# Moving one quarter of the inputs of the eighth step from VectorE to GpSimd in a selective-scan layer

## The chip, the cores and the metric

The kernel runs on one NeuronCore of a Trainium2 chip. Times are device microseconds of one execution of the whole program; "time before" is the median of three runs. The core has TensorE (PE, matrix products into PSUM), VectorE (DVE), ScalarE (ACT), GpSimd (POOL) and SyncE (SP, which here only issues DMA transfers). Each engine works through its own instructions in order and waits on semaphores for the others. SBUF is the working memory of 128 partitions, PSUM the memory that TensorE writes to.

## The reference

The input x has 3 images of 256 channels and 48 x 48 points. Four layers are added to it in turn, each on a group norm of what came before: a block with attention, a convolution with weights mixed from eight experts, a plain convolution, and a selective scan over the 2304 points of each image. Only the last is touched by the change. Cut to what matters:

```python
xz = einsum('blc,dc->bld', layernorm(x), in_proj_w)      # 512 channels d, twice
x_in, z = split(xz, 2)
u = silu(causal_conv4(x_in))
dt_raw, B_ssm, C_ssm = split(einsum('bld,ed->ble', u, x_proj_w))   # 16 + 16 + 16
dt = softplus(einsum('blr,dr->bld', dt_raw, dt_proj_w) + dt_proj_b)
A = -exp(A_log)                                          # 512 x 16
def step(hst, inp):                                      # hst: 512 channels x 16 states
    dA = exp(dt_t[:, :, None] * A)
    hst = hst * dA + dt_t[:, :, None] * B_t[:, None, :] * u_t[:, :, None]
    y_t = einsum('bdn,bn->bd', hst, C_t)
y = (ys + u * D_param) * silu(z)
out = x + einsum('bld,cd->blc', y, out_proj_w)
```

## The kernel before

The program computes the four layers one after the other. The scan layer takes the last two fifths of the time, from about 2008 us on. All numbers are fp32.

**Chunks and steps.** The points of the three images are cut into 18 chunks of 384 (`CH`). A chunk goes through eight steps: four blocks `m` of 128 channels, times two halves `h` of the states. A step holds 128 channels and 8 states, laid out as 128 partitions = 32 channels x 4 states, and along the free dimension a tile `hs` of 2 groups of states `g` x 4 quarters of channels `q` x 384 points. The first step of a chunk is m = 0, h = 0; the eighth is m = 3, h = 1. So the seventh step is m = 3, h = 0.

**A step on each engine.**

- Fills: every (g, q) of `hs` first gets the input of the recurrence, the product dt·u (a quarter of the channels, spread over the partitions) times B. Quarters 0 and 1 are written by VectorE in `fill_upper` (L1765), which reads dt·u from a PSUM tile `ps_r` into which TensorE spread it (`spread_pe`, L1730). One piece, (g, q) = (1, 1) of each second step (h = 1), is written by GpSimd instead (L1779), which reads dt·u from an SBUF tile `dtuq` that DMAs fill (`spread_second`, L1722, a single buffer). Quarters 2 and 3 are written by GpSimd for both groups at once (L1783), from `dtur`, which DMAs fill too (`spread`, L1714, together with `dtr`, the spread dt).
- Decays: ScalarE computes exp(dt·A) for one (g, q) at a time into one of three PSUM slots `ps_da` (L1809).
- Scans: VectorE runs the recurrence over 384 points in place, one (g, q) at a time (L1817), eight scans a step in the order (0,0), (0,1), (1,0), (1,1), (0,2), (0,3), (1,2), (1,3). These are the parts 0 to 7. The decay of part n + 3 is issued behind the scan of part n and needs its slot free.
- GpSimd multiplies the whole `hs` by C into `hc` (`times_c`, L1834; in the very last step VectorE does this, L1828), TensorE sums over the states (`add_states`, L1846 and L1851), and VectorE multiplies by silu(z) (`gate`, L1858).

**Order around the change.** Between two steps the loop issues `fill(s + 1)`, then `times_c(s)`. At a step with h = 0, `fill` has two instructions for VectorE: both groups of that step (128x1536) and already group 0 of the following step (128x768). At a step with h = 1 there is one left for VectorE, (1, 0) (128x384), and L1779 for GpSimd. Then comes L1783 in either case. So VectorE fills for the eighth step in two places: group 0 ahead of the seventh step, (1, 0) ahead of the eighth. `hs` has three buffers, so that GpSimd can fill ahead while VectorE still scans the step before.

A list written out by hand (`plan`, `after`, `gating`) places the preparation of the next two chunks and the output of the one before into half-steps and places within them. Among it are dt·u of the next chunk (`softplus` on ScalarE, L1327 to L1329, and `take_dt` on VectorE, L1343 and L1344, in the sixth and the seventh step), the normalising of the chunk after it (L1246, in the eighth) and the store of the last chunk's output (L1384). `keep_busy` (L1336) issues products on TensorE whose result nobody reads. `first_states` and `last_states` (L1792, L1799) carry states between chunks. At the end of the layer `keep_order` pins the instructions of TensorE, VectorE, ScalarE and GpSimd to the order in which they are written; SyncE is not among them.

The call `fill_upper(s, lo, hi, nq)` covers the groups lo to hi - 1 and the quarters 0 to nq - 1; `b_rows` gives the rows of B for them, each repeated for the quarters. In the code, `chunks[at].second[m]` is `dtuq` and `chunks[at].bc[0]` holds B for the four groups of a channel block, two for each half.

Of the kernel before, what the change touches and what calls it, by code (L numbers as in the profile page):

```python
# [12 lines left out]
ALU = mybir.AluOpType  # L13
# [3 lines left out]
P = 128  # L17
# [8 lines left out]
CH = 384  # L26
# [9 lines left out]
DI = 4  # L36
# [48 lines left out]
def net(  # L85
# [295 lines left out]
    with ExitStack() as l0:  # L381
# [36 lines left out]
        with ExitStack() as p1:  # L418
# [15 lines left out]
            for b in ORDER:  # L434
# [3 lines left out]
                for ct in range(CT):  # L438
                    for j in range(parts):
                        at = slice(j * N // parts, (j + 1) * N // parts)  # L440
# [608 lines left out]
        chunks = [(b, c) for b in ORDER for c in range(NCH)]  # L1049
# [58 lines left out]
    rooms, w3v, chunks, stored = {}, {}, {}, set()  # L1108
# [580 lines left out]
    with ExitStack() as l3:  # L1689
# [60 lines left out]
        def states(s):  # L1750

            if s not in tiles:
                t = scn.tile([P, 2, 4, CH + 4], F32, name="hs", bufs=3)
                tiles[s] = t[:, :, :, 1 : CH + 2]
            return tiles[s]

        def b_rows(s, lo, hi, nq=2):
            at, m, h = steps[s]
            rows = chunks[at].bc[0][:, 2 * h + lo : 2 * h + hi, :]
            return rows.unsqueeze(2).broadcast_to([P, hi - lo, nq, CH])  # L1760

        def fill_upper(s, lo, hi, nq=2):

            k = chunks[steps[s][0]]
            nc.vector.tensor_tensor(  # L1765
                states(s)[:, lo:hi, 0:nq, 1:],
                k.ps[:, 0:nq, :CH].unsqueeze(1).broadcast_to([P, hi - lo, nq, CH]),
                b_rows(s, lo, hi, nq), ALU.mult,
            )

        def fill(s):

            at, m, h = steps[s]
            if h == 0:
                fill_upper(s, 0, 2)
                fill_upper(s + 1, 0, 1)
            else:
                fill_upper(s, 1, 2, 1)
                nc.gpsimd.tensor_tensor(  # L1779
                    states(s)[:, 1, 1, 1:], chunks[at].second[m],  # L1780
                    chunks[at].bc[0][:, 3, :], ALU.mult,
                )
            nc.gpsimd.tensor_tensor(  # L1783
                states(s)[:, :, 2:4, 1:],
                chunks[at].rows[m][1].unsqueeze(1).broadcast_to([P, 2, 2, CH]),
                b_rows(s, 0, 2), ALU.mult,
            )
# [77 lines left out]
        spread_pe(k, 0)  # L1865
        first_states(0)
        fill(0)
        for n in range(3):
            decay(n)
        for s, (at, m, h) in enumerate(steps):  # L1870
# [30 lines left out]
            if s + 1 < len(steps):  # L1901
                fill(s + 1)
# [133 lines left out]
```

## Time and profile before

| What | us |
|---|---|
| median of three runs | 3374.56 (3373.8 to 3378.72) |
| the profiled execution | 3369.03 |
| its span, first to last instruction | 3367.3 |
| busy in the span: TensorE, VectorE | 3151.7 (94%), 2899.6 (86%) |
| busy in the span: ScalarE, GpSimd | 2375.1 (71%), 1335.3 (40%) |
| scans (L1817), 1152 of 936 ns | 1002.6 busy |
| fills by GpSimd of quarters 2 and 3 (L1783), 144 | 418.3 |
| products with C on GpSimd (L1834), 143 | 805.3 |
| fills by GpSimd of (1, 1) (L1779), 72 | about 62 |

Lines of groups give the line of the kernel, the engine, the operation, the tile written and the tiles read, the form and the count, then busy time, the mean of one in ns, and the idle time of that engine just before. Lines of the order in time give start, length, engine, line and operation; a bracket at the end is idle time before it and whose result ended it. Instructions of one kind that follow each other are merged (x2, x6). Lines of waits give who waited for whom, the total in us, how often, and the longest. Consecutive instructions of VectorE overlap by nearly a tenth of a microsecond, so that a scan listed with 936 ns comes every 0.87 us. Tiles that share a room of a former tile appear under two names (`x` or `bc`, `wconv`, `u`).

### The profile page before, as it was taken

The page shows a single profiled execution, that of the slowest core. Times are in us where ns is not written, and L with a number is a line of the kernel's source. Part 1 is how long each engine was busy: PE and PEld are TensorE (multiplying, and loading weights), DVE is VectorE, ACT ScalarE, POOL GpSimd, SP SyncE. Part 2 cuts the span into 40 slices and gives each one's busy share as a digit, 9 for nine tenths or more (in the row PEclk, how much of TensorE's full clock was granted, in tenths as well). Part 3 has the DMA queues.
Part 4 walks back from the last instruction along what each step waited for, and adds up shares of the span by engine and source line. Part 5 has one row for each costly group of instructions (what it writes and reads, how often), then busy time and mean ns, then how long its engine had stood idle before and what let it go on. Part 6 is the DMA issues. An engine that isn't in the chain of part 4 may idle for free.

```text
span 3367.3 us, 54979 instructions
## 1 busy us (share of the span) xinstructions
PE 3151.7 (94%) x21314; PEld 1586.5 (47%) x21314; DVE 2899.6 (86%) x3302; ACT 2375.1 (71%) x3596; POOL 1335.3 (40%) x457
## 2 busy tenths in 40 slices
PE   7999999999999999979999988999999999999985
PEld 4334343452333434547777764444444444444442
DVE  4799989959988997379976459999999999999997
ACT  3688888838888886332233548888888888888874
POOL 0000000000000000220000009999999999999997
PEclk9999999999999999989999999999999999999998
DMA  4000000010000002566611044555545555555552
GB/s 174 23 8 10 8 8 6 8 46 4 8 7 8 10 8 71 193 210 214 218 38 38 19 120 107 125 127 129 143 123 141 133 129 123 130 130 134 135 131 56
DMA packets 182165, 290.84 MB, mean 86 GB/s; under 512 B 34738, under 2 KB 148466, under 8 KB 179971
## 3 DMA queue, kind: packets, MB, share of 16 engines
q1 hardware_dynamic: 168658, 267.15, 29.6%
q10 hardware_dynamic: 13232, 20.06, 1.8%
q8 instruction: 169, 2.77, 0.4%
q14 instruction: 106, 0.86, 0.1%
HBM read 236.24 MB, written 50.64 MB: 85 GB/s over the span
## 4 chain that ended last, share of the span: by engine, by line
PE 52%; DVE 32%; ACT 7%; DMA 4%; issue 4%; SPq 1%; POOL 0%; ACTq 0%; DVEq 0%; POOLq 0%
DVE hs L1817 21%; PE ps_s L638 16%; PE acc L651 14%; PE ps_c L1546 8%; DVE hs L1765 3%; DVE u L296 2%; PE ps_y L462 2%; PE ps_m L665 2%; ACT ps_da L1809 2%; PE ps_s L1031 2%; PE ps_m L711 1%; PE acc L529 1%; PE ps_s L518 1%; DVE ps_g L1343 1%; DMA dtr<-dtd 1%
## 5 line engine op out<-in xcount | busy, mean ns | idle before, releaser
L642 ACT ACTIVATE pt<-ps_s 128x1024 f32<-128x1024 f32 x972 | 942.4, 1022 | 154.8 <-PE ps_s L638 142.1
L1817 DVE TENSOR_TENSOR_SCAN hs<-ps_da,hs 128x385 f32<-128x385 f32 x1152 | 1002.6, 936 | 5.1 <-ACT ps_da L1809 2.4
L857 DVE TENSOR_TENSOR part<-part,pt 128x2048 f32<-128x2048 f32 x396 | 906.6, 2289 | 41.2 <-ACT pt L642 18.5
L1809 ACT ACTIVATE ps_da<-dtr,u 128x384 f32<-128x384 f32 x1152 | 656.3, 582 | 191.3 <-DVE hs L1817 182.7
L164 POOL TENSOR_TENSOR rstd<-ve,mhalf 128x2 f32<-128x2 f32 (+1 forms) x26 | 16.3, 629 | 1473.4 <-DVE ve L162 1473.4
L638 PE MATMUL ps_s<-q,kt 32*128 32x512 f32 (+1 forms) x4320 | 576.4, 592 | 0.1
L651 PE MATMUL acc<-pt,vt 128*32 128x512 f32 (+1 forms) x4320 | 520.9, 561 | 0.2
L1546 PE MATMUL ps_c<-vt,u 128*128 128x288 f32 x1728 | 429.4, 409 | 21.0 <-DVE u L263 21.0
L1834 POOL TENSOR_TENSOR hc<-hs,x 128x3072 f32<-128x3072 f32 x72 | 405.2, 5628 | 30.8 <-DVE hs L1817 26.0
L1834 POOL TENSOR_TENSOR hc<-hs,bc 128x3072 f32<-128x3072 f32 x71 | 400.1, 5635 | 24.7 <-DVE hs L1817 23.0
L1546 PEld LDWEIGHTS ps_c<-vt,u 128*128 128x128 f32 x1728 | 328.9, 191 | 116.6 <-issue 19.8
L638 PEld LDWEIGHTS ps_s<-q,kt 32*128 32x128 f32 x4320 | 195.3, 183 | 199.1 <-issue 120.2
L651 PEld LDWEIGHTS acc<-pt,vt 128*32 128x32 f32 x4320 | 94.4, 108 | 353.4 <-issue 326.7
L1851 PE MATMUL ps_y<-hc,u 128*32 128x384 f32 x2304 | 228.1, 516 | 2.8 <-POOL hc L1834 2.8
L1273 PE MATMUL ps_g<-u 128*128 128x384 f32 x576 | 196.2, 494 | 23.4 <-ACT u L1269 23.4
L1783 POOL TENSOR_TENSOR hs<-dtur,x 128x1536 f32<-128x1536 f32 x72 | 209.0, 2903 | 8.3 <-DMA dtur<-dtud 8.3
L1783 POOL TENSOR_TENSOR hs<-dtur,bc 128x1536 f32<-128x1536 f32 x72 | 209.3, 2907 | 1.3 <-DMA dtuq<-dtud 0.9
L1273 PEld LDWEIGHTS ps_g<-u 128*128 128x128 f32 x576 | 108.8, 191 | 107.7 <-ACT u L1269 34.6
L1336 PE MATMUL ps_r<-hs,ident 128*128 128x128 f32 x864 | 130.9, 292 | 27.3 <-DVE hs L1817 27.2
L1336 PEld LDWEIGHTS ps_r<-hs,ident 128*128 128x128 f32 x864 | 107.6, 192 | 80.8 <-DVE hs L1817 63.0
L1851 PEld LDWEIGHTS ps_y<-hc,u 128*32 128x32 f32 x2304 | 62.0, 112 | 144.5 <-issue 130.4
L1562 ACT COPY cb<-ps_c 128x288 f32<-128x288 f32 x48 | 19.1, 398 | 154.5 <-PE ps_c L1546 140.4
(266 smaller groups left out, 4051.0 us busy)
## 6 DMA issues: line engine op xcount, KB each, us to landing
wconv<-in_we SPq DMA_DIRECT2D x144, 384.0 KB, 4.2
dtr<-dtd SPq DMA_DIRECT2D x288, 192.0 KB, 3.9
dtur<-dtud SPq DMA_DIRECT2D x288, 96.0 KB, 4.3
wconv<-xd SPq DMA_DIRECT2D x36, 384.0 KB, 3.7
x<-bcd SPq DMA_DIRECT2D x72, 192.0 KB, 5.1
dtd<-x SPq DMA_DIRECT2D x36, 384.0 KB, 2.9
dtuq<-dtud SPq DMA_DIRECT2D x288, 48.0 KB, 2.0
bc<-bcd SPq DMA_DIRECT2D x72, 192.0 KB, 4.8
```

Source lines behind the costliest of these rows:

```text
L638: nc.tensor.matmul(s[:, j, cols], kt[r, mt * P : (mt + 1) * P], q[r, :n], start=True, stop=True,)
L642: nc.scalar.activation(p[:, h0 : h0 + 2, :], s, AF.Exp)
L651: nc.tensor.matmul(acc[h * HD : (h + 1) * HD, :n], vt[:, mt, g * P + h * HD : g * P + (h + 1) * HD], p[:, h, cols], start=mt == 0, stop=mt ...
L857: ): nc.vector.tensor_tensor(part, first, p, ALU.add)
L1273: nc.tensor.matmul(bank[m % 2], w3v["taps"][:, m, tap, :], w3v["xi"][:, m % 3, tap : tap + CH], start=tap == 0, stop=tap == DCONV - 1,)
L1336: nc.tensor.matmul(spread_tiles[-1][:, i % 2, CH:], ident, src, start=True, stop=True)
L1546: nc.tensor.matmul(pc[:, :HN], u[:, i, dy, ct, m * P : (m + 1) * P], vt[:, i, ct, dy * TW : dy * TW + HN], start=ct == 0 and dy == 0, stop ...
L1783: nc.gpsimd.tensor_tensor(states(s)[:, :, 2:4, 1:], chunks[at].rows[m][1].unsqueeze(1).broadcast_to([P, 2, 2, CH]), b_rows(s, 0, 2), ALU.mult,
L1809: nc.scalar.activation(slots[n % 3][:, 1 : CH + 1], chunks[at].rows[m][0][:, q, :], AF.Exp, scale=amat[:, col : col + 1],)
L1817: nc.vector.tensor_tensor_scan(b, slots[(8 * s + part) % 3][:, : CH + 1], b, 0.0, ALU.mult, ALU.add)
L1834: nc.gpsimd.tensor_tensor(hc, tiles[s][:, :, :, 1:], cb.broadcast_to([P, 2, 4, CH]), ALU.mult)
L1851: nc.tensor.matmul(k.y_ps[32 * q : 32 * q + 32, :CH], fold, hc[:, g, q, :], start=False, stop=h == 1 and g == 1,)
```

## The change

At the eighth step of each chunk GpSimd fills the second quarter of channels (q = 1) for both groups of states, and VectorE fills only the first. The piece that changes hands is (g, q) = (0, 1), 384 elements in each partition. The call for VectorE ahead of the seventh step covers one quarter instead of two when m is the last block; the instruction for GpSimd ahead of the eighth step covers both groups. At the other steps with h = 1 it covers one group as before, written with a group dimension of one.

```diff
             if h == 0:
                 fill_upper(s, 0, 2)
-                fill_upper(s + 1, 0, 1)
+                fill_upper(s + 1, 0, 1, 1 if m == DI - 1 else 2)
             else:
                 fill_upper(s, 1, 2, 1)
+                lo = 0 if m == DI - 1 else 1
                 nc.gpsimd.tensor_tensor(
-                    states(s)[:, 1, 1, 1:], chunks[at].second[m],
-                    chunks[at].bc[0][:, 3, :], ALU.mult,
+                    states(s)[:, lo:2, 1, 1:],
+                    chunks[at].second[m].unsqueeze(1).broadcast_to([P, 2 - lo, CH]),
+                    chunks[at].bc[0][:, 2 + lo : 4, :], ALU.mult,
                 )
```

## The prediction

> **What bounds the kernel now.** I read the busy shares over the span first, then the totals of one chunk of the scan layer, VectorE's waits there, and the order of time around the edit on VectorE, GpSimd and ScalarE. The edit lies in the scan layer, from about 2008 us to the end. In 40 slices of 84.2 us:
>
> ```profile
> DVE  4799989959988997379976459999999999999997
> ACT  3688888838888886332233548888888888888874
> POOL 0000000000000000220000009999999999999997
> ```
>
> In slices 25 to 39 VectorE and GpSimd both show 9 tenths, so the average of GpSimd over the span (40%) says nothing about its room there. One chunk (eight steps) by itself, from one step's first scan to the same scan a chunk later:
>
> ```profile
> core 0: us, PE busy (x) PEld busy (x) DVE busy (x) ACT busy (x) POOL busy (x), PEclk, DMA share, GB/s
> 2536.79:2611.08 74.29, 68.59 (x348) 36.01 (x347) 73.67 (x90) 62.43 (x123) 71.06 (x21) 1.00 0.55 132
> ```
>
> VectorE is busy 73.67 of 74.29 us, GpSimd 71.06: 0.6 us of room against 3.2. The chunk repeats at 74.3 us (2091.11, 2165.42, 2239.71 and so on). Over sixteen such chunks (2091 to 3278 us) the list of waits has only these for VectorE:
>
> ```profile
> DVE hs L1765 <- ACT wconv L1384: 3.4, 16, 0.2
> DVE ps_g L1343 <- ACT x L1329: 2.8, 16, 0.2
> DVE hs L1817 <- issue: 0.4, 1, 0.4
> ```
>
> That is 0.2 us twice a chunk, none of it for GpSimd. VectorE sets the pace; what it drops counts in full unless something lies within that distance behind it. The place of the edit, in one chunk, on VectorE:
>
> ```profile
> 2514.01 2.62 DVE L1765 TENSOR_TENSOR hs<-ps_r,x 128x1536 f32<-128x1536 f32 x2
> 2516.54 1.80 DVE L1817 TENSOR_TENSOR_SCAN hs<-ps_da,hs 128x385 f32<-128x385 f32 x2
> 2518.25 0.54 DVE L1343 SCALAR_TENSOR_TENSOR ps_g<-ps_g,x 128x384 f32<-128x384 f32 x1
> ...
> 2525.48 0.53 DVE L1765 TENSOR_TENSOR hs<-ps_r,x 128x384 f32<-128x384 f32 x1
> 2525.93 5.40 DVE L1817 TENSOR_TENSOR_SCAN hs<-ps_da,hs 128x385 f32<-128x385 f32 x6
> ```
>
> The first line is the two fills ahead of the seventh step: 1536 elements for that step, 768 for the eighth. The same stretch on GpSimd:
>
> ```profile
> 2513.81 5.63 POOL L1834 TENSOR_TENSOR hc<-hs,x 128x3072 f32<-128x3072 f32 x1 [0.28 <-PE ps_r L1336]
> 2519.40 0.86 POOL L1779 TENSOR_TENSOR hs<-dtuq,x 128x384 f32<-128x384 f32 x1
> 2520.22 2.90 POOL L1783 TENSOR_TENSOR hs<-dtur,x 128x1536 f32<-128x1536 f32 x1
> 2525.74 5.63 POOL L1834 TENSOR_TENSOR hc<-hs,x 128x3072 f32<-128x3072 f32 x1 [2.62 <-DVE hs L1817]
> ```
>
> To be seen: L1779 is the operation that grows, and 2.62 us of GpSimd's 3.2 us of idle time come right behind it, waiting for the seventh step's last scan.
>
> **What the Trainium skill says.** "GPSIMD Engine Reference", 3.1 (Elementwise), gives about 1 cycle an element on VectorE and about 2.6 on GpSimd for an operation with two inputs. At the clocks of the two pages' Specifications (0.96 and 1.2 GHz) that is an estimate of 0.40 us for 384 elements on VectorE and 0.83 on GpSimd. The trace gives 0.418 and 0.68 (below), and these are used. "VectorE: DVE Perf Modes", "Why PSUM operands drop a tier", says that an fp32 operation with a PSUM operand stays at one element a cycle; the fill reads ps_r from PSUM, and 1.05 to 1.09 ns an element agrees. "GPSIMD Engine Reference", 8 (Key points), says that GpSimd contends with VectorE's two-port modes or two SBUF inputs. Scans and fills have one input in PSUM, so more GpSimd time beside them should cost nothing. The trace agrees: the six scans from 2520.37 take 5.20 us, 0.867 each, although GpSimd is busy until 2523.1 and idle after it, and scans fully under GpSimd work keep that pitch.
>
> **The change, part by part.** All of it happens once a chunk, and there are 18 chunks.
>
> *Removed from VectorE.* The second of the two fills (L1765, for the eighth step) goes from 128x768 to 128x384. The view of that line gives 948 ns as its median, which is the 768 form, and 530 as its minimum, the 384 form, so 0.418 us go; from start to start, about 0.86 (2515.7 to 2516.54) less 0.45 (2525.48 to 2525.93) gives 0.41. I take 0.418. The fill ahead of the eighth step (0.53) stays.
>
> *Added to GpSimd.* L1779 goes from 384 to 768 elements. Its own kind of operation costs 865 ns for 384, 2903 for 1536 and 5628 for 3072: (2903 - 865)/1152 = 1.77 ns an element in both steps. So 865 + 384 x 1.77 = 1.54 us, 0.68 more. At the second, fourth and sixth step of a chunk the operation keeps its size and only gets a dimension of one, costed at nothing (at worst some tens of ns, under the same idle time).
>
> *What hides the 0.68.* L1779 starts at 2519.40, ends at 2520.94 instead of 2520.26; L1783 ends at 2523.8 instead of 2523.12. The next operation, L1834, waits for the scan that ends at 2525.5, now 2525.1. So 2.62 - 0.68 - 0.42 = 1.5 us of cover remain; without them, the 0.68 would delay all GpSimd work up to the next chunk.
>
> *Who waits for L1779.* The new part, group 0 second quarter, is scanned as part 1 of the eighth step, at 2525.93 - 0.42 + 0.87 = 2526.4, 5.4 us after 2520.94. L1783's quarters are first due at part 4, at about 2529.0, 5.2 us after 2523.8. No new wait ends there.
>
> *Does the 0.42 get through?* Behind the fill, ScalarE is the nearest:
>
> ```profile
> 2515.96 0.84 ACT L1329 ACTIVATE x<-x 128x768 f32<-128x768 f32 x1
> 2516.71 0.19 ACT L1799 COPY gmat<-hs 128x8 f32<-128x8 f32 x1
> 2517.52 0.58 ACT L1809 ACTIVATE ps_da<-dtr,u 128x384 f32<-128x384 f32 x1 [0.62 <-DVE hs L1817]
> ```
>
> ScalarE waits 0.62 us for the first scan, so it can follow by 0.42 with 0.2 to spare; this wait is 0.62 to 0.72 in all of the first 17 chunks. VectorE's L1343, due at 2517.83 instead of 2518.25, needs L1329, done at 2516.80: 1.0 left. From there ScalarE's decays, TensorE's products and the transfers start from VectorE's results and shift with it, also the two 0.2 us waits, whose ScalarE strings start from waits of 0.26 for a scan. SyncE's queue has the same issues; its L1722 for the next chunk comes at 2527.5, long after L1779 has let go of its only buffer.
>
> *The last chunk* has no preparation of a following one, VectorE is quicker there, and GpSimd works without a gap: L1779 from 3336.54, L1783 from 3337.36, L1834 from 3340.23. With the change L1783 ends at 3336.54 + 1.50 + 2.91 = 3340.95. Part 4 would be due at 3337.67 - 0.42 + 3.46 = 3340.7, now waits for about 3341.0; before it was 3341.1. So 0.1 of the 0.42 remains. L1834 then ends at 3346.5, just ahead of the products at 3346.64 that read it.
>
> *Sum.* 17 x 0.418 + 0.1 = 7.2 us. The profiled execution took 3369.03 us (span 3367.3 and 1.7 around it) and would take 3361.8. The median of the three runs, 3374.56, lies 5.5 above it; I carry the same 7.2 over: 3367.4 us, 0.21% faster.
>
> **The rivals.** *Taken up on the way*: ScalarE has only 0.2 us left behind the fill, and waits of 0.2 on it already stand twice a chunk. If one of its strings were fixed by something else than a scan, a transfer say, VectorE would merely wait longer there. For it: those waits. Against: each string starts from a wait for VectorE. All lost gives 3374.6, half lost 3371.
>
> *Slower, by a wait for VectorE's own fill*: the new L1779 writes one quarter of each of two groups, and between them in memory lies group 1's first quarter, which VectorE fills at 2525.48, ordered ahead of it. If the write counted as one block, L1779 would wait until 2525.6. Then part 1, due at 2526.4, waits for 2527.2, and part 4, due at 2529.8 after that, for L1783 at 2530.05: 0.8 + 0.25 = 1.05 us lost against 0.42 won. That makes +0.63 x 17 = 11 us: 3385. GpSimd would be 4.7 us late too, which its margins of 4 to 5 us just take. It decides from the first overlap counted. Against it: L1783's write spans that very quarter as well and starts at 2520.22 without waiting.
>
> *A longer GpSimd operation* hurts only from 0.68 + 1.5 = 2.2 us of growth, three times the estimate. *Another order of transfers*: SyncE's order isn't among the four that the kernel pins. The tightest transfer, dtr, lands at 2529.3 and ScalarE needs it at 2531.7; beyond 2.4 us a swap would cost, at 1 us a chunk 17 - 7 = 10 us, 3385 again. *That the edit does nothing* is out: it cuts a row with a measured length.
>
> **How the numbers follow.** The forecast has 0.72. Its size lies between 17 x 0.40 = 6.8 and 18 x 0.45 = 8.1 with run noise of about 1 us around it. Taken up wholly or half has 0.15, the wait for the fill 0.08, the other slower ways 0.05. A measurement of this kernel tells about 0.2% (6.75 us) from no change. Four fifths of the forecast's 0.72 lie beyond: faster 0.58; the rest and the absorbed case: same 0.29; slower 0.13. The range goes from 3365 (8.1 and noise) to 3375 (all absorbed).
>
> **What would show it.** Right: the chunk at 73.9 us; L1765 with 54 operations of 128x768 and 90 of 128x384; L1779 at about 1.54 us once a chunk, and the wait of 2.62 us shrunk to 1.5. Wrong: L1779 starting after VectorE's fill, an idle VectorE before part 1 or 4 of the eighth step, or the 0.2 us waits grown to 0.6.

## The result and the profile after

The changed kernel took 3363.81 us (median of 8 executions, 3361.71 to 3369.11) against 3373.61 us of the kernel before beside it (8 executions, 3368.78 to 3378.72). The ratio is 0.9973, with a 95% interval from 0.9964 to 0.9983: 9.1 us faster, between 5.7 and 12.1 (the two medians by themselves are 9.8 apart). That is faster, as forecast, by a little more than the 7.2 us forecast. The median was forecast at 3367.4 us, in a range from 3365 to 3375, and lies 1.2 us below that range.

The profiled execution shows none of it: 3369.11 us, span 3367.4, where the kernel before had 3369.03 and 3367.3. So the time has to be read by stage. The scan layer's first fill (L1765) starts at 2016.82 us in the profile after and at 2008.33 in the one before, although nothing ahead of it was edited; from there to the end it takes 1350.6 against 1359.0 us.

A chunk first. The view of busy times by stretch for the changed kernel, from part 3 of the sixth step (behind `take_dt`) to the same scan a chunk later (columns: stretch, length, busy time of TensorE, its weight loads, VectorE, ScalarE and GpSimd, granted clock, DMA share, GB/s):

```profile
core 0: us, PE busy (x) PEld busy (x) DVE busy (x) ACT busy (x) POOL busy (x), PEclk, DMA share, GB/s
2514.21:2588.11 73.90, 69.35 (x346) 36.09 (x346) 73.28 (x90) 62.45 (x123) 71.70 (x21) 0.98 0.57 135
```

73.90 us where it was 74.29. VectorE has 0.4 us less of work and the same 0.6 us idle, GpSimd 0.6 more. The waits of VectorE over 2091 to 3278 us, same kernel:

```profile
DVE hs L1765 <- ACT wconv L1384: 3.4, 16, 0.2
DVE ps_g L1343 <- ACT x L1329: 2.9, 16, 0.2
DVE hs L1819 <- issue: 0.4, 1, 0.4
```

They are what they were. No new wait has come, and the two of 0.2 us haven't grown. The order in time around the edit, on VectorE, then GpSimd, then ScalarE (lines of the code have moved on by one or two: L1780 is the former L1779, L1785 was L1783, L1819 was L1817, L1811 was L1809, L1836 was L1834):

```profile
2518.93 2.21 DVE L1765 TENSOR_TENSOR hs<-ps_r,x 128x1536 f32<-128x1536 f32 x2
2521.05 1.80 DVE L1819 TENSOR_TENSOR_SCAN hs<-ps_da,hs 128x385 f32<-128x385 f32 x2
2522.77 0.54 DVE L1343 SCALAR_TENSOR_TENSOR ps_g<-ps_g,x 128x384 f32<-128x384 f32 x1
...
2530.45 5.39 DVE L1819 TENSOR_TENSOR_SCAN hs<-ps_da,hs 128x385 f32<-128x385 f32 x6
```

```profile
2518.73 5.63 POOL L1836 TENSOR_TENSOR hc<-hs,x 128x3072 f32<-128x3072 f32 x1 [0.27 <-PE ps_r L1336]
2524.31 1.54 POOL L1780 TENSOR_TENSOR hs<-dtuq,x 128x768 f32<-128x768 f32 x1
2525.81 2.90 POOL L1785 TENSOR_TENSOR hs<-dtur,x 128x1536 f32<-128x1536 f32 x1
2530.25 5.63 POOL L1836 TENSOR_TENSOR hc<-hs,x 128x3072 f32<-128x3072 f32 x1 [1.53 <-DVE hs L1819]
```

```profile
2520.88 0.84 ACT L1329 ACTIVATE x<-x 128x768 f32<-128x768 f32 x1
2521.63 0.19 ACT L1801 COPY gmat<-hs 128x8 f32<-128x8 f32 x1
2522.04 0.58 ACT L1811 ACTIVATE ps_da<-dtr,u 128x384 f32<-128x384 f32 x1 [0.22 <-DVE hs L1819]
```

The two fills take 2.21 instead of 2.62 us. L1780 takes 1.54 us and starts right behind the operation ahead of it, so it doesn't wait for VectorE's fill of the quarter in between, which comes at 2530.00. GpSimd's wait has gone from 2.62 to 1.53, ScalarE's from 0.62 to 0.22.

### The profile page after: what moved, and what is told of

It reads as the page before. It is cut to its first block, busy times and chain, and to the rows that moved or that the text cites. A ratio compares the mean times of both kernels' runs of the same rounds, so it can differ in the third digit from the quotient of the medians.

```text
span 3367.4 us, 54979 instructions
## 1 busy us (share of the span) xinstructions
PE 3159.9 (94%) x21314; PEld 1591.0 (47%) x21314; DVE 2892.8 (86%) x3302; ACT 2376.1 (71%) x3596; POOL 1346.1 (40%) x457
## 4 chain that ended last, share of the span: by engine, by line
PE 52%; DVE 32%; ACT 7%; DMA 5%; issue 4%; SPq 1%; POOL 0%; ACTq 0%; DVEq 0%; POOLq 0%
DVE hs L1819 21%; PE ps_s L638 16%; PE acc L651 14%; PE ps_c L1546 8%; DVE hs L1765 3%; PE ps_s L1031 2%; DVE u L296 2%; PE ps_y L462 2%; ACT ps_da L1811 2%; PE ps_m L665 1%; PE ps_m L711 1%; PE acc L529 1%; PE ps_s L518 1%; DVE ps_g L1343 1%; PE ps_s L578 1%
## 5 line engine op out<-in xcount | busy, mean ns | idle before, releaser
L1819 DVE TENSOR_TENSOR_SCAN hs<-ps_da,hs 128x385 f32<-128x385 f32 x1152 | 1002.1, 935 | 4.2 <-ACT ps_da L1811 1.5
L1811 ACT ACTIVATE ps_da<-dtr,u 128x384 f32<-128x384 f32 x1152 | 656.6, 582 | 184.3 <-DVE hs L1819 175.7
L1836 POOL TENSOR_TENSOR hc<-hs,x 128x3072 f32<-128x3072 f32 x72 | 405.3, 5629 | 19.2 <-DVE hs L1819 15.2
L1836 POOL TENSOR_TENSOR hc<-hs,bc 128x3072 f32<-128x3072 f32 x71 | 399.9, 5633 | 15.9 <-DVE hs L1819 14.2
L1785 POOL TENSOR_TENSOR hs<-dtur,x 128x1536 f32<-128x1536 f32 x72 | 209.2, 2905 | 9.1 <-DMA dtur<-dtud 8.5
L1785 POOL TENSOR_TENSOR hs<-dtur,bc 128x1536 f32<-128x1536 f32 x72 | 209.3, 2907 | 1.1 <-DMA dtuq<-dtud 1.1
L1336 PE MATMUL ps_r<-hs,ident 128*128 128x128 f32 x864 | 130.7, 292 | 19.8 <-DVE hs L1819 19.5
L1336 PEld LDWEIGHTS ps_r<-hs,ident 128*128 128x128 f32 x864 | 107.6, 192 | 73.8 <-DVE hs L1819 56.1
```

The costliest lines, as they stand in the source:

```text
L1336: nc.tensor.matmul(spread_tiles[-1][:, i % 2, CH:], ident, src, start=True, stop=True)
L1785: nc.gpsimd.tensor_tensor(states(s)[:, :, 2:4, 1:], chunks[at].rows[m][1].unsqueeze(1).broadcast_to([P, 2, 2, CH]), b_rows(s, 0, 2), ALU.mult,
L1811: nc.scalar.activation(slots[n % 3][:, 1 : CH + 1], chunks[at].rows[m][0][:, q, :], AF.Exp, scale=amat[:, col : col + 1],)
L1819: nc.vector.tensor_tensor_scan(b, slots[(8 * s + part) % 3][:, : CH + 1], b, 0.0, ALU.mult, ALU.add)
L1836: nc.gpsimd.tensor_tensor(hc, tiles[s][:, :, :, 1:], cb.broadcast_to([P, 2, 4, CH]), ALU.mult)
```

## The experiments

Each chunk but the last two contains one normalising on VectorE (L1246, in the eighth step). The steps between these marks give the pace free of what lies ahead of the layer. Times in us, one profile each; the last column is the length that most chunks share:

| kernel | first fill at | first fill to first mark | 15 chunks, first to last mark | last mark to the end | common chunk |
|---|---|---|---|---|---|
| before | 2008.33 | 77.24 | 1114.57 | 167.16 | 74.30 |
| before, again | 2008.74 | 75.92 | 1114.53 | 167.01 | 74.30 |
| changed | 2016.82 | 75.71 | 1108.52 | 166.35 | 73.89 |
| changed, again | 2012.37 | 75.64 | 1108.48 | 166.11 | 73.89 |
| GpSimd's part alone | 2010.42 | 75.72 | 1114.53 | 166.53 | 74.30 |
| sixth and eighth step | 2007.35 | 76.81 | 1108.37 | 167.47 | 73.90 |
| the same without silu | 2016.73 | 75.19 | 1102.30 | 166.68 | 73.48 |
| fourth step only | 2011.76 | 77.42 | 1114.21 | 167.61 | 74.30 |
| second and eighth step | 2010.55 | 75.45 | 1102.57 | 166.93 | 73.50 |
| all four | 2010.73 | 76.91 | 1104.42 | 168.74 | 73.3 to 75.1 |
| GpSimd's fill twice | 2011.30 | 75.63 | 1108.71 | 167.36 | 73.91 |
| GpSimd's fill four times | 2012.29 | 76.75 | 1146.79 | 177.27 | 76.47 |

**The same two kernels again.** No edit.

> The changed kernel once more. Theory S (steady): the change is worth 0.41 us in each of 18 chunks, some 7.3 us, and what was measured beyond that (9.1 us, from the ratio 0.9973) is spread between executions of the stages ahead of the scan layer and of the layer's start. Then the chunk is 73.90 us again, the sixteen chunks and the tail repeat to 0.2 us, the start of the scan layer lies anywhere within some 10 us, and the ratio lies between 0.9970 and 0.9985. Theory M (more): the other 2 us belong to the change, through the start of the layer. Then the time from the first fill to the first normalising is 75.7 us here again, against 77.2 in every profile of the kernel before, and the ratio stays at or below 0.9973.

> The kernel before once more, compared with itself: the spread by itself. Theory S: chunk 74.30 us, ratio 1.000 with an interval of about 0.001 to each side; the first fill of the scan layer moves by several us against the first profile (2008.3 us) although nothing was edited, and the stretch from it to the first normalising moves by about 1 us. Theory M: that stretch is 77.2 us again.

Measured: the changed kernel 3365.07 us (18 executions), ratio 0.9978, interval 0.9971 to 0.9985, which is 7.4 us; the kernel before against itself 0.9999, interval 0.9991 to 1.0007 (13 executions against 54). The 54 executions of the kernel before spread over 10.8 us (3367.71 to 3378.55), and one of the 13 beside them lay lower still, at 3364.63. The chunk and the fifteen chunks repeat to 0.05 us in either kernel, while the layer's start moved by 4.5 us in the changed kernel with no edit at all. The first stretch, 77.24 in the first profile of before, is 75.92 in the second. Theory M falls by that stretch; the ratio alone wouldn't decide it, as its interval reaches from 5 to 10 us. No stage of the profiles gives what went beyond 7.3 us in the first comparison to the change.

**GpSimd's part alone.**

```diff
-                fill_upper(s + 1, 0, 1, 1 if m == DI - 1 else 2)
+                fill_upper(s + 1, 0, 1)
```

(against the changed kernel: VectorE fills the quarter too, as before, GpSimd keeps the larger fill)

> GpSimd fills the second quarter of both groups in the eighth step as in the change, and VectorE fills it too, as before. Theory S: the 0.68 us more on GpSimd is under its wait for the seventh step's last scan, so the chunk stays at 74.30 us and the ratio is 0.999 to 1.001. Rival (the longer GpSimd operation costs something, which hides part of a larger gain on VectorE): chunk above 74.4 us, ratio above 1.001.

Measured: 3372.96 us, ratio 0.9999, interval 0.9990 to 1.0007, chunk 74.30. GpSimd's wait for the seventh step's last scan is 1.92 us, 0.69 less than before. The added work on GpSimd costs nothing measurable; by difference, the whole gain is VectorE's 0.41 us.

**Also in the sixth step.**

```diff
-                fill_upper(s + 1, 0, 1, 1 if m == DI - 1 else 2)
+                fill_upper(s + 1, 0, 1, 1 if m >= 2 else 2)
...
-                lo = 0 if m == DI - 1 else 1
+                lo = 0 if m >= 2 else 1
```

> The change in the sixth step as well as in the eighth. GpSimd has no idle time of its own behind its fill there. Theory S, with the limit that ScalarE sets: GpSimd's total of about 72.4 us a chunk is still under VectorE's, and its lateness of 0.68 us is inside its margin of 4 us, so GpSimd costs nothing; but from the end of the fourth step ScalarE works for some 9 us without a wait for a scan (table loads and silu) and then waits only 0.27 us, so of the 0.41 us about 0.27 gets through: chunk about 73.6 us, 12 us under the kernel before, ratio about 0.9964, and VectorE's wait of 0.17 at L1343 grows to about 0.3. Rival G (a moved fill pays only where GpSimd idles right behind it): nothing gained in the sixth step, chunk 73.9 or more. Rival V (only VectorE's time counts): chunk 73.49 us.

Measured: 3366.13 us, ratio 0.9978 (0.9972 to 0.9985), chunk 73.90. All of the sixth step's 0.41 us is lost, where 0.27 was expected to get through, and the time and the place of the loss differ from what theory S said. On VectorE, in the fifth step:

```profile
2491.01 2.21 DVE L1765 TENSOR_TENSOR hs<-ps_r,x 128x1536 f32<-128x1536 f32 x2
2493.13 2.65 DVE L1819 TENSOR_TENSOR_SCAN hs<-ps_da,hs 128x385 f32<-128x385 f32 x3
2496.10 4.36 DVE L1819 TENSOR_TENSOR_SCAN hs<-ps_da,hs 128x385 f32<-128x385 f32 x5 [0.32 <-ACT ps_da L1811]
```

and on ScalarE beside it:

```profile
2490.67 0.58 ACT L1811 ACTIVATE ps_da<-dtr,u 128x384 f32<-128x384 f32 x1 [0.26 <-DVE hs L1819]
2491.28 1.28 ACT L1286 ACT_TABLE_LOAD   x1
2492.57 1.49 ACT L1286 ACTIVATE u<-u 128x1536 f32<-128x1536 f32 x1
2494.08 1.28 ACT L229 ACT_TABLE_LOAD   x1
2495.37 0.20 ACT L1801 COPY gmat<-hs 128x8 f32<-128x8 f32 x1
2495.48 1.08 ACT L1811 ACTIVATE ps_da<-dtr,u 128x384 f32<-128x384 f32 x2
```

ScalarE starts table load, silu and table load behind a decay that waits for the fourth step's scans, and comes to part 3's decay only at 2495.48. VectorE's fill lies between that start and part 3, so its being shorter doesn't make the decay earlier: VectorE waits 0.32 us for it, and the rest is the overlap of two scans that follow each other, some 0.08 us, which a wait between them undoes. The same place in the changed kernel's second profile:

```profile
2497.43 6.92 DVE L1819 TENSOR_TENSOR_SCAN hs<-ps_da,hs 128x385 f32<-128x385 f32 x8
2499.38 1.08 ACT L1811 ACTIVATE ps_da<-dtr,u 128x384 f32<-128x384 f32 x2
```

The first of the two decays is part 3's. It is done at 2499.96 us, and VectorE gets to part 3 at 2500.00: there was nothing left to win behind the string. The wait sits here and not at L1343, as theory S had it. GpSimd isn't among VectorE's waits, so rival G has the number right for another reason; the next two runs tell them apart.

**The same with silu left out.** The entry for the silu of u is taken out of the plan, so later chunks scan a u without silu.

```diff
-        (7, LATE, 1, lambda k: silu(k.u)),
```

> The change in the sixth and the eighth step, with the silu of u (and its two table loads) left out of the plan of the fourth half of a chunk, so that chunks behind the first scan a u without silu. Theory S: the string on ScalarE that took the sixth step's gain is gone, VectorE's wait for ps_da of 0.3 us is gone, and the chunk is 73.4 to 73.5 us. Theory G (GpSimd has no idle time behind its sixth fill): 73.9 us still.

Measured: 3362.6 us in one execution, chunk 73.48; the list of VectorE's waits has no ps_da any more. With ScalarE's string gone, the sixth step's 0.41 us comes through in full, though GpSimd has no idle time behind its fill there, as before. Rival G falls here. The kernel without silu but without the two moves wasn't run; that it would gain nothing by itself is read from the list of waits of the kernel before, which has no ps_da.

**In the fourth step instead.**

```diff
-                fill_upper(s + 1, 0, 1, 1 if m == DI - 1 else 2)
+                fill_upper(s + 1, 0, 1, 1 if m == 1 else 2)
...
-                lo = 0 if m == DI - 1 else 1
+                lo = 0 if m == 1 else 1
```

> The fill moved in the fourth step instead of in the eighth. Theory S: silu on ScalarE (1.3 us of table load, 1.5 of silu, 1.3 of table load) starts with the end of the second step whatever VectorE saves, and the decay of part 3 of the third step comes last as it is (VectorE's eight scans there take 7.02 us against 6.90 elsewhere). So the 0.41 us saved between turn into a wait of VectorE for ps_da, and the chunk stays at 74.30 us. Theory V (only VectorE's time counts): 73.89 us. Theory G: 74.3 us, but with VectorE waiting for GpSimd.

Measured: 3372.76 us in one execution, chunk 74.30. VectorE's waits in sixteen chunks, which begin with a new one:

```profile
DVE hs L1819 <- ACT ps_da L1811: 4.6, 16, 0.3
DVE hs L1765 <- ACT wconv L1384: 3.4, 16, 0.2
```

In one chunk, in the third step:

```profile
2485.70 4.47 DVE L1819 TENSOR_TENSOR_SCAN hs<-ps_da,hs 128x385 f32<-128x385 f32 x5 [0.31 <-ACT ps_da L1811]
```

It is part 3 again, whose decay (from 2485.09) comes behind a table load, silu and table load on ScalarE. The same edit, two blocks of channels earlier than in the eighth step, saves VectorE as much work and the kernel nothing. Theory V falls.

**In the second step and in the eighth.**

```diff
-                fill_upper(s + 1, 0, 1, 1 if m == DI - 1 else 2)
+                fill_upper(s + 1, 0, 1, 1 if m in (0, DI - 1) else 2)
...
-                lo = 0 if m == DI - 1 else 1
+                lo = 0 if m in (0, DI - 1) else 1
```

> The change in the second step as well as in the eighth. Behind the end of a chunk ScalarE waits 1.05 us for the first scan, so it can follow VectorE by 0.41 us, and its next long string (table loads and silu) starts from a wait for a scan. Theory S (VectorE's time counts unless ScalarE's string fixes the time behind it; GpSimd only by its total and its margin of 4 to 5 us): all 0.41 us of the second step count, chunk 73.49 us, ratio about 0.9957. Rival G (a moved fill pays only where GpSimd idles at least 0.68 us right behind it; behind the second step's fill it idles 0.40 us): chunk 73.9 us, ratio about 0.998, VectorE waiting for GpSimd.

Measured: 3359.29 us (3357.22 to 3363.29, 6 executions), ratio 0.9959, interval 0.9947 to 0.9971; chunk 73.50, GpSimd busy 72.32 us of it. This beats both kernels. In the last chunk, which has no preparation of a following one, it also shows a stall of the kind that the prediction had worked out for part 4 in the last chunk of the change itself:

```profile
3324.51 0.95 DVE L1819 TENSOR_TENSOR_SCAN hs<-ps_da,hs 128x385 f32<-128x385 f32 x1
3326.06 2.66 DVE L1819 TENSOR_TENSOR_SCAN hs<-ps_da,hs 128x385 f32<-128x385 f32 x3 [0.59 <-POOL hs L1780]
3328.92 3.51 DVE L1819 TENSOR_TENSOR_SCAN hs<-ps_da,hs 128x385 f32<-128x385 f32 x4 [0.21 <-POOL hs L1785]
```

Part 1 waits for GpSimd's piece of quarter 1, part 4 for the quarters 2 and 3.

**In all four steps with h = 1.**

```diff
-                fill_upper(s + 1, 0, 1, 1 if m == DI - 1 else 2)
+                fill_upper(s + 1, 0, 1, 1 if True else 2)
...
-                lo = 0 if m == DI - 1 else 1
+                lo = 0 if True else 1
```

> The fill moved in the second, fourth, sixth and eighth step. VectorE alone, with ScalarE's two strings, would make 73.50 us as with the second and the eighth. GpSimd's total is 70.98 + 4 x 0.68 = 73.7 us. Theory S: GpSimd becomes the bound, chunk 73.7 to 74.0 us, VectorE waiting for GpSimd's fills, so two moves more lose against two moves. If GpSimd's size never counts: 73.50 us.

Measured: 3362.53 us in one execution, 73.63 us a chunk on the mean (1104.42 over 15), a little under what was expected. A stretch of it:

```profile
2500.00:2574.00 74.00, 69.02 (x348) 36.26 (x349) 72.64 (x91) 62.82 (x126) 74.00 (x21) 1.00 0.55 132
```

GpSimd has no idle time left. The first chunks still run at 73.50, on the lead that GpSimd's fills have; as it falls behind, chunks of 73.6 follow and one of 75.07, with a wait of 1.38 us of VectorE for a product (L1336) in it. Behind that one the last five run at 73.3 to 73.5 again. VectorE waits for GpSimd's fill (L1780) six times, 1.9 us in all, as expected. So the two further moves win nothing and use up GpSimd.

**GpSimd's fill of the eighth step twice, and four times.**

```diff
-                nc.gpsimd.tensor_tensor(
+                for _ in range(2 if m == DI - 1 else 1):
+                    nc.gpsimd.tensor_tensor(
```

(the operation itself is only indented; 4 in place of 2 in the second kernel)

> The changed kernel with GpSimd's fill of the second quarter of the eighth step done twice, about 1.55 us more on GpSimd; its wait of 1.53 us for the seventh step's last scan should be gone or nearly so. The prediction said that a longer operation there hurts only from 1.5 us more on. Theory S: total about 73.3 us, still under the pace, chunk 73.9 us. Rival (any GpSimd growth beyond the cover is paid at once by the scans of the eighth step): chunk above 74.0 us.

> The changed kernel with GpSimd's fill of the second quarter of the eighth step done four times over, 4.5 us more on GpSimd a chunk. Its total is then 71.7 + 4.5 = 76.2 us against VectorE's 73.3. Theory S: GpSimd sets the pace, chunk about 76.2 us, some 39 us (1.2%) over the changed kernel, ratio about 1.009, with VectorE waiting for L1785's fills. If GpSimd's fills were free whatever their size: chunk 73.9 us.

Measured: twice, 3364.74 us in one execution, chunk 73.91, as in the changed kernel, and the wait of 1.53 us is gone. Four times, 3415.05 us, ratio 1.0122 (1.0106 to 1.0138), chunk 76.47. There L1781 (the fill, four in a row) takes 6.43 us, and the scans wait for it:

```profile
2540.05 0.94 DVE L1820 TENSOR_TENSOR_SCAN hs<-ps_da,hs 128x385 f32<-128x385 f32 x1
2542.92 2.66 DVE L1820 TENSOR_TENSOR_SCAN hs<-ps_da,hs 128x385 f32<-128x385 f32 x3 [1.93 <-POOL hs L1781]
```

So GpSimd's fills aren't free at any size: GpSimd's total decides. It is 71.7 us with the change; 1.6 us more was still covered, and 4.9 us more makes 76.6, about the chunk of 76.47.

## Why the prediction was right in its mechanism and where its number fell short

*What is removed.* Forecast 0.418 us a chunk; measured 0.41 in the two fills (2.62 to 2.21) and 0.40 in the chunk (74.30 to 73.89; 1114.55 to 1108.50 over fifteen chunks, 6.05 us).

*What is added, and its cover.* Forecast 1.54 us for L1779 and 1.5 us of its cover left; measured 1.54 and 1.53. GpSimd's part alone costs nothing, twice the fill neither, four times the fill does. The limit named, 1.5 us of further growth, was tried at 1.6 us (nothing lost) and at 4.9 (lost), not in between.

*Whether it gets through.* Forecast: ScalarE keeps 0.2 us behind the fill; measured 0.22. The rival "taken up on the way" was wrong for this step and right for the steps beside it: the fourth and the sixth step's 0.41 us go to ScalarE's table loads and silu whole. The reason given against it, that each string on ScalarE starts from a wait for VectorE, doesn't exclude it: the string starts from a scan *ahead* of the shortened fill and is needed behind it. The prediction was right here because in the seventh step a wait of ScalarE for a scan lies directly behind the fill.

*A wait for VectorE's own fill.* Didn't come: L1780 starts at 2524.31, VectorE's fill at 2530.00.

*The last chunk.* Forecast 0.1 us; it gave nearly all of its 0.4. The last mark to the end includes two shortened fills and went from 167.1 to 166.2, while VectorE's last product with C moved from 144.79 behind the mark to 144.0. The working took GpSimd's place against VectorE from the profile of before, with a wait of 0.36 us of L1783 for dtur (at 3274.91) in it. That wait is not there in the profile after, nor in the second profile of the kernel before, so GpSimd reached L1780 1.11 us ahead of the scans (3336.67 against 3337.78) instead of 0.7, and L1785's end at 3341.06 came just ahead of part 4 at 3341.2.

*The sum.* 18 x 0.403 = 7.3 us instead of 7.2. The repeated comparison has 7.4.

*What failed* is the size given to run noise, the last term of "How the numbers follow". The range's lower end, 3365, is 3374.56 less 8.1 us of gain, less "run noise of about 1 us". The gain, 7.3 us, stayed inside its term. But from 3374.56 down to the measured 3363.81 are 10.8 us, so 3.5 us aren't the gain, where about 1 was allowed. Of these, 1.0 lies in the starting point: 3374.56 is a median of three, and 54 executions of that kernel have 3373.53. Another 1.3 lies at the other end: 3363.81 is a median of eight, and 18 executions of the same kernel have 3365.07. The last 1.2 is what these two larger medians, 8.5 us apart, still differ from 7.3. Executions of one kernel spread over 11 us here, so medians of three and of eight wander by a microsecond and more. The repeat's 3365.07 would have fallen just inside the range; that the first comparison did not is chance and no property of the kernel. The first comparison came out 1.8 us over the steady gain, which its own interval (5.7 to 12.1 us) covers. The spread arises mostly ahead of the edited layer: its first fill started between 2007.35 and 2016.82 us in twelve profiles, while from there to the end the four with a chunk of 74.30 us took 1356.8 to 1359.3. What makes the start vary wasn't tried and stays open.

## What to carry to other kernels

A shortened piece of work pays only as far as the next thing behind it that was started by something ahead of it: look on each other engine for the last wait *before* the shortened piece, and follow its string from there to the first result needed *after* it. The same edit gave 0.4 us in the second and the eighth step of one loop and nothing in the fourth and the sixth. For a gain of a few tenths of a per cent compare repeated stages in the profile, which repeat to hundredths of a microsecond here, and take the spread for the range from the whole time, which doesn't.

## What the runs showed of the hardware that was not expected

The time of the whole program spread by 10.8 us over 54 executions, while fifteen chunks of the scan layer repeated to 0.05 us in 1114. Larger GpSimd fills beside the scans left their pitch alone, which had been expected: eight scans of a step took 6.90 us in the kernel with the second and the eighth step moved (GpSimd busy 72.32 of 73.50 us) as in the kernel before, and from start to start a scan took 0.85 us in both, not the 0.87 us given ahead of the change. The prediction's 0.867 us is a listed length divided by its number of scans, with the whole of the last scan in it.
